# Attention projections: seven-product Strassen in float32 against three-pass Karatsuba in float32r, on one core

## The chip, the cores and the metric

The kernel runs on one core of one Trainium2 chip. The metric is the device time of one execution in microseconds (us). A core has a matrix engine (TensorE, in the profile PE, with its weight loads as PEld), a vector engine (VectorE, DVE), an engine for activation functions (ScalarE, ACT), a general engine (GpSimd, POOL) and SyncE (SP), which here only issues DMAs. Each of them works through its own queue in order and waits for others by semaphores. Matrix products land in PSUM[...] and are read out from there by VectorE or ScalarE; all other tiles lie in SBUF.

## The reference

64 graphs share one adjacency matrix `a` of 256 x 256 nodes; `x` is 64 x 256 x 512, float32. Two layers, each with a residual and a layer norm:

```python
# layer 0
mi = x @ Wi.T ; mj = x @ Wj.T
x = layernorm(x + deg * (mi + b) + a @ mj)
# layer 1
q, k, v = x @ Wq.T + bq, x @ Wk.T + bk, x @ Wv.T + bv      # 8 heads of 64
attn = softmax(where(a == 0, -inf, q @ k.T / 8))
x = layernorm(x + (attn @ v) @ Wo.T + bo)
```

Each of the four weights of layer 1 is 512 x 512. Per graph, each of these projections is a product of 256 x 512 with 512 x 512.

## The kernel before

**Batches in pairs.** The loop (`for g in range(NG - 1)`, L986) runs 31 times, with two graphs ("batches") per turn: it does the attention of pair `g`, layer 0 of pair `g + 1`, the output projection `o` of pair `g`, and q, k, v of pair `g + 1`. Layer 0 of the first pair and its q, k, v stand ahead of the loop; the attention and the output of the last pair follow it.

**Layer 0** (`l0_steps`, L502) is a Strassen scheme over the two row tiles and two halves of the channels: seven products per batch, each of two float32 matmuls with 512 columns, in the banks `x`, `w`, `y` and `z`. The left factors are the transposed input `xT` (`turn_x`, a VectorE transpose) and its four combinations `xS` (`sum_x`, L494). Steps 5 to 7 give `mj`, which is split into a float32r head `hi` (ScalarE) and a rest `lo` (GpSimd). `neighbours` multiplies both by the adjacency matrix `graph`, in eight float32r matmuls per batch, into the two banks of `pa`. `take` adds the result to `xh` and begins the norm, `give` applies it.

**h is turned through DRAM.** `send_h` (L599) writes the two row tiles of the normed rows to DRAM in two DMAs; after the second one it issues the read of the whole batch into `hB`. `turn_h` (L610) transposes 128 x 1024 at once on VectorE into `hT`, and for the second batch forms the four combinations `hS`.

**Projections before** (`pair_steps`, L650; `block_product`, L640). The two batches of a pair are the two row blocks of a Strassen scheme: seven products, each of four float32 matmuls with 256 columns, for each of q, k, v (`qkv_steps`, L675) and o (`o_steps`, L737). The right factors are 128 x 512 blocks or combinations of blocks (256 KB each), made once ahead of the loop (`make_factors`, L412), kept in DRAM and streamed in by `bring` (L438) through a ring of nine buffers; a factor that has been used is replaced by the next at once. Products are evicted by ScalarE (copies) and joined by VectorE and GpSimd (`u1`, `u2`, `u3`).

**Attention.** A slot `w` is a pair of heads of one batch. `scores` (L795) computes scores for a slot (4 matmuls) and returns a function that adds the mask (VectorE, L809), takes the exponential (ScalarE, L813) and adds the two key tiles for the denominators (GpSimd, L816). `values` (L830) multiplies by v. `divide_two` (L850) copies two slots out and calls `divide` (L875): denominators by a matmul with ones, the reciprocal (VectorE, L886), eight small DMAs that spread the reciprocals over the partitions, and a running sum `rtot` on GpSimd. `multiply` (L845) applies them on GpSimd later.

**PSUM.** `score_banks` are two buffers of two banks each; they hold scores, and `pa` of the neighbour sum. `value_bank` is one bank, and `bank` is a pool of three. Together they are all eight.

**What sets the order.** Instructions given to `in_order` (L282) keep the order of the program on their engine; that holds for all matmuls. The others are placed by the compiler's scheduler. Before, many of VectorE's and GpSimd's instructions were free in this sense, the mask add among them. Matmuls are all recorded under L290, their helper's line.

## Time and profile before

| | |
|---|---|
| median of 3 runs | 3070.68 us (3068.39 to 3071.82) |
| the profiled execution | 3068.79 us |
| its span in the profile | 3066.9 us |
| granted TensorE clock, mean | 0.999 of full |
| weights and activations moved by DMA | 447.54 MB, 146 GB/s on average |
| DMA queue of SyncE, share of 16 engines | 48.8% |

The costliest groups of TensorE, by name of the tile written and the tiles read (a float32 matmul is two records, so counts are twice the number of matmuls; busy times overlap with those of neighbours):

| group | shape | records | busy us |
|---|---|---|---|
| layer 0, `po` from `w0` and `xS` or `xT` | 128 x 512 | 1792 | 814.3 |
| projections, `st` from `factor` and `hS`, `hT`, `oS` or `aoT` | 128 x 256 | 7112 | 1625.1 |
| scores, `ps` | 64 x 256 | 2048 | 265.0 |
| values, `pav` | 128 x 256 | 4096 | 248.4 |
| neighbour sum, `pa` | 128 x 512, float32r | 512 | 212.2 |

In the views below a row of a timeline has the start in us from the beginning of the span, the length, the engine, the line, the operation, output and inputs, the shape, and the number of records that were merged into the row. Brackets name the time that the engine was idle before it, and what ended it. A row of the waits names who waited, for whom, the total, the number of times and the longest one.

### The profile page before, as it was taken

What the parts mean: (1) busy time and instruction counts of PE and PEld (TensorE: products, weight loads), DVE (VectorE), ACT (ScalarE), POOL (GpSimd) and SP (SyncE); (2) the same over time, 40 slices, a digit from 0 to 9 for tenths busy, and PEclk for the clock granted to TensorE, in tenths of its full rate; (3) what the DMA queues carried; (4) which work ended last, traced back from release to release, by engine and by line L of the source; (5) the groups of instructions that cost most, each with busy time, mean ns of one, the idle gap of its engine ahead of it and who ended that gap; (6) DMA issues with size and microseconds to landing.
All of it is one profiled execution on the core that took longest, in us unless ns stands there. A gap on an engine that the chain in (4) does not pass through costs nothing. (4 is left out here: it accounts for less than half of the span.)

```text
span 3066.9 us, 46810 instructions
## 1 busy us (share of the span) xinstructions
PE 3036.6 (99%) x16646; PEld 2124.6 (69%) x16646; DVE 2178.3 (71%) x3298; ACT 974.1 (32%) x1861; POOL 1519.5 (50%) x1255
## 2 busy tenths in 40 slices
PE   7999999999999999999999999999999999999998
PEld 4667766677766777666776667776677766677665
DVE  6776677766777667777677777677766777767775
ACT  2323333323333333332233332333333333323332
POOL 2544545544545445464454554454544546445453
PEclk9999999999999999999999999999999999999999
DMA  7455544455444555345553445544455444555333
GB/s 255 123 151 159 169 121 136 132 161 166 144 125 127 159 170 155 116 133 154 161 168 119 126 145 160 167 134 134 127 158 170 151 121 128 159 161 166 120 111 96
DMA packets 410411, 447.54 MB, mean 146 GB/s; under 512 B 40896, under 2 KB 300224, under 8 KB 409792
## 3 DMA queue, kind: packets, MB, share of 16 engines
q1 hardware_dynamic: 410176, 444.50, 48.8%
q8 instruction: 136, 2.23, 0.3%
q14 instruction: 99, 0.81, 0.1%
HBM read 340.79 MB, written 70.25 MB: 134 GB/s over the span
## 5 line engine op out<-in xcount | busy, mean ns | idle before, releaser
L461 POOL TENSOR_TENSOR rstd<-ve,mhalf 128x1 f32<-128x1 f32 x256 | 140.5, 552 | 707.3 <-DVE below L459 707.3
L816 POOL TENSOR_TENSOR pk<-pe 128x512 f32<-128x512 f32 x256 | 323.1, 1278 | 322.2 <-ACT pe L813 322.2
L290 PE MATMUL po<-w,xS 128*128 128x512 f32 x1024 | 462.2, 599 | 0.7 <-DVE xS L478 0.7
L290 PE MATMUL st<-hS,factor 128*128 128x256 f32 x2048 | 453.2, 379 | 1.5 <-DVE u L689 1.2
L290 PEld LDWEIGHTS st<-hS,factor 128*128 128x128 f32 x2048 | 388.4, 190 | 56.3 <-DVE xh L744 1.7
L813 ACT ACTIVATE pe<-pe 128x1024 f32<-128x1024 f32 x256 | 270.8, 1058 | 364.4 <-DVE pe L809 364.4
L290 PE MATMUL po<-w,xT 128*128 128x512 f32 x768 | 352.1, 601 | 14.8 <-DVE xS L477 9.3
L290 PE MATMUL st<-hT,factor 128*128 128x256 f32 x1536 | 352.5, 379 | 0.7 <-ACT hT L626 0.7
L290 PEld LDWEIGHTS po<-w,xS 128*128 128x128 f32 x1024 | 189.6, 190 | 235.6 <-issue 206.3
L809 DVE TENSOR_TENSOR pe<-ps,maskT 128x1024 f32<-128x1024 f32 x256 | 298.0, 1195 | 35.4 <-PE ps L290 35.4
L290 PEld LDWEIGHTS st<-hT,factor 128*128 128x128 f32 x1536 | 291.9, 190 | 41.8 <-ACT hT L626 0.9
L886 DVE RECIPROCAL rden<-den 128x256 f32<-128x256 f32 x127 | 222.5, 1752 | 76.6 <-PE den L290 73.6
L290 PEld LDWEIGHTS po<-w,xT 128*128 128x128 f32 x768 | 144.2, 191 | 181.9 <-issue 162.8
L887 POOL TENSOR_TENSOR rtot<-rtot,rden 128x256 f32<-128x256 f32 x127 | 106.8, 841 | 320.1 <-DVE rden L886 320.1
L290 PE MATMUL ps<-qT,kT 64*128 64x256 f32 x2048 | 265.0, 393 | 0.0
L290 PE MATMUL pav<-pe,v_sb 128*32 128x256 f32 x4096 | 248.4, 382 | 1.9 <-ACT pe L813 1.9
L290 PEld LDWEIGHTS ps<-qT,kT 64*128 64x128 f32 x2048 | 184.5, 186 | 78.1 <-issue 38.6
L744 DVE TENSOR_TENSOR xh<-st,xh 128x512 f32<-128x512 f32 x186 | 144.5, 777 | 132.2 <-PE st L290 132.2
L290 PE MATMUL st<-factor,hS 128*128 128x256 f32 x1024 | 234.8, 382 | 0.0
L290 PEld LDWEIGHTS pav<-pe,v_sb 128*32 128x32 f32 x4096 | 119.8, 110 | 164.3 <-issue 95.4
L290 PE MATMUL st<-factor,oS 128*128 128x256 f32 x992 | 224.2, 379 | 0.0
L290 PEld LDWEIGHTS st<-factor,hS 128*128 128x128 f32 x1024 | 192.1, 190 | 35.2 <-issue 10.6
(115 smaller groups left out, 4648.2 us busy)
## 6 DMA issues: line engine op xcount, KB each, us to landing
xB<-in_x_dram SPq DMA_DIRECT2D x256, 128.0 KB, 3.9
xh<-in_x_dram SPq DMA_DIRECT2D x64, 512.0 KB, 4.2
factor<-wq SPq DMA_DIRECT2D x128, 256.0 KB, 4.2
factor<-wk SPq DMA_DIRECT2D x128, 256.0 KB, 2.8
factor<-wv SPq DMA_DIRECT2D x128, 256.0 KB, 2.6
spread<-rden SPq DMA_DIRECT2D x1016, 32.0 KB, 1.9
factor<-wo SPq DMA_DIRECT2D x124, 256.0 KB, 3.2
h_cols<-xh SPq DMA_DIRECT2D x124, 256.0 KB, 3.0
```

Source lines behind the costliest of these rows:

```text
L290: in_order(nc.tensor.matmul(*args, **kw))
L461: nc.gpsimd.tensor_tensor(rstd, ve, mhalf, ALU.pow)
L744: nc.vector.tensor_add(dst, src, dst)
L809: nc.vector.tensor_add(pe.rearrange("p j t q -> p j (t q)"), ps.rearrange("p j t q -> p j (t q)"), maskT.rearrange("p t q -> p (t q)").uns ...
L813: in_order(nc.scalar.activation(flat, flat, AF.Exp, scale=QSCALE, accum_out=etot[:, NB * g + i, pr:pr + 1]))
L816: nc.gpsimd.tensor_tensor(pk, pe[:, :, 0, :], pe[:, :, 1, :], ALU.add)
L886: nc.vector.reciprocal(rden, den)
L887: nc.gpsimd.tensor_tensor(rtot, rtot, rden, ALU.add)
```

## The change

Its parts:

- **Projections in three float32r passes.** Each activation is split into a head, a low part and a difference (`split_head` on ScalarE, `split_low` on GpSimd, `split_diff` on VectorE), and each weight likewise (`make`): head, lifted low part, difference. The product is `X = head*head + low*lift` and `Y = diff*diff`; the result is `UP * X + Y`. Every projection is thus three products of full size, of float32r matmuls with 512 columns: 48 per projection and pair, and nothing is combined over the two batches. `hS`, `oS` and the keepers `u1` to `u3` go.
- **Weights** come in 16 chunks per turn (four for each weight) of 128 x 3 x 512, 786 KB each, through a ring of `RING = 6` buffers. Ahead of the loop a chunk is made by ScalarE and VectorE from the raw weight and stored.
- **Banks.** Each product takes a pair of banks (`pair`): "S" one of the two score buffers, "M" two of the pool of three, "A" one of these and the value bank.
- **v in pairs** (`v_pair`): both row tiles of a batch go through chunk by chunk. o goes row tile by row tile for the first batch, and in a pair for the second.
- **h in halves.** Each row tile is sent (`send_h`), fetched (`fetch_h`) and turned (`turn_h`) by itself.
- **Order.** Nearly every instruction is now given to `in_order`, and the loop's body is written out. Steps 1 to 4 of the next layer 0 are moved into the turn before.
- **Smaller ones.** `mj` is added by VectorE from PSUM instead of a copy and an add on GpSimd; the second `lo` of a batch is VectorE's; `rtot` is summed by ScalarE; the heads' channels are laid out so that `divide` needs four DMAs instead of eight.

The core of the diff:

```diff
-    AHEAD = 8
+    RING = 6
+    UP, DOWN, LIFT = 1 + 2.0 ** -12, 1 - 2.0 ** -13, 2.0 ** 12
...
+    def make(f, name, j):
+        head, lift, diff = (f[:, i, :].rearrange("p (c o) -> p c o", c=NC) for i in range(3))
+        low = p3.tile([P, NC, P], F32, tag="lu", name="low")
+        for cs, raw in pieces(name, j):
+            in_order(nc.scalar.activation(head[:, cs], raw, AF.Identity, scale=DOWN))
+            in_order(nc.vector.tensor_sub(low[:, cs], raw, head[:, cs].bitcast(F32)))
+            in_order(nc.scalar.activation(lift[:, cs], low[:, cs], AF.Identity, scale=LIFT))
+        in_order(nc.vector.scalar_tensor_tensor(diff, low, LIFT, head.bitcast(F32), ALU.mult, ALU.subtract))
+        nc.sync.dma_start(out=kept[name][j], in_=f.bitcast(F32))
...
+    def split_head(parts, src):
+        in_order(nc.scalar.activation(parts[0], src, AF.Identity, scale=DOWN))
+
+    def split_diff(parts, src):
+        in_order(nc.vector.scalar_tensor_tensor(parts[2], parts[0].bitcast(F32), UP, src, ALU.mult, ALU.subtract))
+
+    def split_low(parts, src, engine):
+        in_order(engine.tensor_tensor(parts[1], src, parts[0].bitcast(F32), ALU.subtract))
...
+    def pair(kind):
+        if kind == "S":
+            both = score_banks("pxy")
+            return both[:, 0, :], both[:, 1, :]
+        return bank("px"), value_bank("py") if kind == "A" else bank("py")
+
+    def rows_of_product(banks, parts, t, f, c):
+
+        X, Y = banks
+        head, low, diff = (d[:, c, t * P:(t + 1) * P] for d in parts)
+        first, end = c == 0, c == NC - 1
+        matmul(X, head, f[:, 0, :], start=first, stop=False, skip_group_check=True)
+        matmul(Y, diff, f[:, 2, :], start=first, stop=end, skip_group_check=True)
+        matmul(X, low, f[:, 1, :], start=False, stop=end, skip_group_check=True)
...
+    def v_pair(g, i, kinds, last):
+        def run():
+            if g not in vv:
+                vv[g] = p1.tile([P, NB, NT, D], F32, tag="v", name="v_sb")
+            banks = {t: pair(kinds[t]) for t in (1, 0)}
+            for c in range(NC):
+                for t in (1, 0):
+                    rows_of_product(banks[t], hP[g], NT * i + t, coming[0 if last else c], c)
+                if last:
+                    coming.pop(0)
+                    bring()
+            for t in (1, 0):
+                v_evict(g, i, t, banks[t])
+        return run
```

o for the second batch, with the fetches and turns of h inside it (`fetch` and `turn` are `fetch_h` and `turn_h` of the second batch of the next pair):

```diff
+        def two():
+            banks = [pair(kinds[NT + t]) for t in range(NT)]
+            for c in range(NC):
+                for t in range(NT):
+                    rows_of_product(banks[t], parts, NT + t, coming[0], c)
+                coming.pop(0)
+                bring()
+                if c in fetch:
+                    fetch[c]()
+            h1 = turn(1)
+            split_head(*h1)
+            split_low(*h1, nc.gpsimd)
+            add_x(1, 0, banks[0])
+            add_y(1, 0, banks[0])
+            split_diff(*h1)
+            h0 = turn(0)
+            split_head(*h0)
+            split_low(*h0, nc.gpsimd)
+            add_x(1, 1, banks[1])
+            split_diff(*h0)
+            add_y(1, 1, banks[1])
```

The loop's body, first and last thirds (`p` and `q` are the layer-0 steps of batches 1 and 2 of the next pair, counted from 0; `next_scores` computes two slots' scores, adds the mask of the first and returns the rest of the second):

```diff
+        run([p[4], p[5], q[0], p[6]])
...
+        values(g, 0)
+        values(g, 1)
+        sum_x(b2)
+        divide_two(g, 1)
+        next_scores(2)()
+        nb1()
+        add1(1)
+        add1(0)
+        run(q[1:2])
+        stat1(1)
+        run(q[2:3])
+
+        values(g, 2)
+        values(g, 3)
...
+        values(g, 6)
+        values(g, 7)
+        aoP[g][1], = three(("v",))
+        split_low(*ao_parts(g, 0, every), nc.gpsimd)
+        split_low(*ao_parts(g, 1, upper), nc.gpsimd)
+        divide_two(g, 7)
+        if g + 2 < NG:
+            next_p[0][2]()
+        split_diff(*ao_parts(g, 1, upper))
+        nb2()
+        add2(1)
+        add2(0)
+        stat2(1)
+        multiply()
+        split_head(*ao_parts(g, 1, lower))
+        give2(1)
+        send_h(b2, 1)
+        p, q = next_p, next_q
+        v, q_, k = projection_steps(g + 1)
         end = finish_steps(g)
...
+        o[0]()
+        stat2(0)
+        split_diff(*ao_parts(g, 1, lower))
+        split_low(*ao_parts(g, 1, lower), nc.gpsimd)
+        give2(0)
+        send_h(b2, 0)
+        o[1]()
+        run([o[2], v[0]])
+        sum_x(b3)
+        v[1]()
+        turn_x(b3 + 1)
+        run([end[0], q_[0], end[1], k[0], end[2], q_[1], end[3], k[1], end[4]])
...
+        run([q_[2]])
...
+        run([k[2], q_[3]])
+        run([scores(g + 1, 0), scores(g + 1, 1)])
+        if g + 2 < NG:
+            add_bias(b3 + 1)
+            p[0][3]()
+        k[3]()
```

## The prediction, made before the changed kernel was run

> **What bounds the kernel now.** I read the page first, then TensorE's list of waits, then the timeline of one turn of the main loop, engine by engine. From the page (busy time by engine) and from TensorE's waits:

> ```profile
> PE 3036.6 (99%) x16646; PEld 2124.6 (69%) x16646; DVE 2178.3 (71%) x3298; ACT 974.1 (32%) x1861; POOL 1519.5 (50%) x1255
> ...
> PE po L290 <- DVE xS L477: 9.3, 1, 9.3
> ```

> TensorE is busy 99% of the span, and its longest wait comes once, at the start. Busy can flatter (ends of matmuls are modelled), so I take starts instead. TensorE's timeline, with start, length and count of records:

> ```profile
> 1495.70 7.07 PE L290 MATMUL st<-hS,factor 128*128 128x256 f32 x32
> 1502.61 1.89 PE L290 MATMUL st<-factor,hT 128*128 128x256 f32 x8
> ...
> 1534.97 0.50 PE L290 MATMUL pa<-hi,graph 128*128 128x512 f32 x1
> 1535.31 0.40 PE L290 MATMUL pa<-lo,graph 128*128 128x512 f32 x1
> 1535.54 0.40 PE L290 MATMUL pa<-hi,graph 128*128 128x512 f32 x1
> ...
> 1536.72 0.39 PE L290 MATMUL pa<-lo,graph 128*128 128x512 f32 x1
> 1537.04 1.14 PE L290 MATMUL ps<-qT,kT 64*128 64x256 f32 x8
> ...
> 1629.37 0.50 PE L290 MATMUL pa<-hi,graph 128*128 128x512 f32 x1
> ```

> Three readings. One turn (same matmul to same matmul) takes 1629.37 - 1534.97 = 94.40 us. In a projection 32 records take 1502.61 - 1495.70 = 6.91 us, so a record of 256 columns costs 0.216; a float32 matmul is two records, 0.432. The float32r matmuls of the neighbour sum are one record each: (1536.72 - 1535.31) / 6 = 0.235 us for 512 columns. Entering and leaving such a run costs 0.2 more: 1537.04 - 1534.97 = 2.07 against 8 x 0.235 = 1.88.

> TensorE never starves because the others are ready in time, barely. VectorE around this neighbour sum and the next, and SyncE (DMA issue) after it:

> ```profile
> 1506.67 0.42 DVE L479 TENSOR_TENSOR xS<-xT 128x256 f32<-128x256 f32 x1
> ...
> 1534.05 1.76 DVE L886 RECIPROCAL rden<-den 128x256 f32<-128x256 f32 x1 [0.52 <-PE den L290]
> 1535.72 1.16 DVE L809 TENSOR_TENSOR pe<-ps,maskT 128x1024 f32<-128x1024 f32 x1
> 1537.14 0.69 DVE L579 TENSOR_TENSOR xh<-pa,xh 128x512 f32<-128x512 f32 x1 [0.26 <-PE pa L290]
> ...
> 1559.21 0.69 DVE L579 TENSOR_TENSOR xh<-pa,xh 128x512 f32<-128x512 f32 x1 [0.72 <-PE pa L290]
> ...
> 1575.90 2.10 DVE L485 STREAM_TRANSPOSE hT<-hB 128x1024 f32<-128x1024 f32 x1
> ```

> ```profile
> 1564.35 0.38 SPq L603 DMA_DIRECT2D h_cols<-xh  x1
> ...
> 1566.55 0.41 SPq L603 DMA_DIRECT2D h_cols<-xh  x1
> ...
> 1572.00 0.33 SPq L607 DMA_DIRECT2D hB<-h_cols  x1
> ```

> The mask add ends at 1536.88, and the scores that need its PSUM buffer start at 1537.04: no time is lost, because only one score product stands before the neighbour sum. The second neighbour sum ends at 1559.02; its rows go to DRAM, back, and through the transpose that ends at 1578.00: 19.0 us.

> [...] a float32 512-column product takes two records of 0.43 (0.86), the float32r one 0.235. [...] the trace has 216 per float32 pass but 235 for float32r, and I use 235. [...] The kernel owns all eight (two score buffers of two banks, one value bank, three others), so a new product waits for a read of an old one. [...] the last sum of xS took 1.50 us beside GpSimd's lo, 0.42 otherwise.

> **The change, part by part, per turn of the loop (31 turns).**

> 1. TensorE. Removed: four projections x 28 matmuls x 0.432 = 48.35. Added: four x 48 float32r matmuls x 0.235 (0.2335 in the second run) = 44.83. Runs of float32r go from two to three (first neighbour sum; second sum with o, v and most of q and k; the last k step), +0.2. Layer 0, scores, values and denominators keep their counts. Net -3.3 us, if TensorE is fed.

> 2. VectorE. Out: the combinations of hS and oS (8 x 0.69), the recombinations after q, k, v (14 instructions, 8.8), o's adds (4.7). In: one add per q and k step (8 x 0.69), four for v, eight for o, the differences (h 4 x 0.7, attention 4 x 0.7), two lows 1.6. By my sum 68 becomes about 74 us of some 91: not the bound on average. But all of it is now pinned in program order, and TensorE's waits depend on where it stands.

> 3. GpSimd loses mj, rtot and the recombinations and gains lows: 47 to about 43. ScalarE gains heads, evictions and totals: 30 to about 39. Both lie beside TensorE; on the path only at the places below. Uncovered, one low costs 1.4 and one head 0.6.

> 4. First new wait: the first neighbour sum. It now follows both score products of w = 2 and 3, which hold both score buffers, so it waits for the mask add of w = 2. From the turn's start (layer-0 step 5): steps 5, 6, the next batch's step 1 and step 7 take 4 x 1.73 and end at 6.92; values and denominators 9.23; two scores 11.16: TensorE is ready. VectorE: mj 7.1 to 7.75, ScalarE's hi to 8.45, low to 9.15 (pinned, so VectorE waits for hi), sum_x 1.6 to 10.75, reciprocal 1.67 to 12.4, mask add to 13.56. Stall 2.4. Behind it in TensorE's queue stand steps 2 and 3 of the next batch and values(2). Bounds: with sum_x out of the way the reciprocal alone starts at 9.4 and 1.0 is left; with a low stretched by GpSimd 3.2. I take 2.4.

> 5. Second new wait: batch 2's rows of h. After the second neighbour sum come o (48 matmuls), v of batch 1 (24): 72 x 0.235 = 16.9 us, then v of batch 2, which needs h of that batch; before, this chain took 19.0. New in it: the halves shorten the last transpose by 1.05; head, difference and the o evictions between add about 2.5 (0.65 + 0.65 + 0.65 + 0.6); o's second score buffer is freed only by an add queued behind both transposes, so even v's first tile waits for them. ScalarE's give also stands behind a head that waits for GpSimd's multiply. Sum 20.2: stall 3.3. Bounds: 0 if pinned order and earlier fetches of half rows bring the chain under 16.9; 5.5 if the fetch runs behind the new weight chunks (next point). I take 3.2.

> 6. Transfers. Weights: 16 chunks of 786 KB instead of 28 of 262 KB, 12.6 MB instead of 7.3 per turn; the mean goes from 146 to about 210 GB/s, while two-microsecond windows of this trace reach 374. Each q or k step eats a chunk in 2.8 us (279 GB/s), with six in the ring. I take no stall of its own. Spread DMAs fall from eight to four per pair on SyncE (gain on its queue: 4 x 0.6, beside TensorE). xB loads moved out of turn_x move along SyncE's queue, and each bring that waits for its slot holds what is behind it, h's fetches too; that is the upper bound in point 5.

> 7. Start: 12 chunks must be made by ScalarE and VectorE before or during the first projections; the first takes about 2.9 us (0.6 + 0.7 + 0.6 + 1), the next 1.5 each, against v's 0.7 per chunk: some 5 us lost, 2.6 won by three cheaper projections. +3, bounds -3 to +12. The tail keeps its products: 0.

> Sum: 31 x (-3.3 + 2.4 + 3.2) = 31 x 2.3 = +71, +3 at the start. The profiled execution took 3068.79 (span 3066.9); it becomes about 3143. The median is 1.9 above it, within the spread of the runs; I rounded the two stalls down a little and forecast 3140 for the median.

> **Rivals.**
> - Forecast (0.50): both new waits cost more together than the 3.3 won. 3085 to 3185.
> - The stream stays fed (0.25, faster): the h chain fits into 16.9 us, and only part of the first stall stays, 1.0. 31 x (-3.3 + 1.0) + 3 = -68: about 3002; with no stall at all 2971. For: TensorE waited for nothing in the middle of the trace, and SyncE's queue is shorter. Against: 19.0 us measured for the chain. Where both stalls together come under 3.3 us a turn, this side decides.
> - Weight transfers become the bound (0.20): h's write, fetch and the ring collide with 786 KB chunks, 2 us more a turn: 3140 + 62 = 3202. For: 302 to 374 GB/s in busy windows already; against: six chunks in the ring.
> - Gain and stalls cancel (0.05): 3070.

> **How the numbers follow.** A difference under 0.2% (6 us) can't be told from none. Faster 0.25 (the second case), same 0.04 (most of the last), slower 0.71 (first, third, rest). Predicted 3140. Low end 3005: it keeps half of the fed case, leaving about 0.11; high end 3205 leaves about 0.09. The likeliest case's own range is 3085 to 3185.

> **What would show it.** The float32r records of the projections 0.235 apart (point 1); turn length from neighbour sum to neighbour sum near 96.7; TensorE idle some 2.4 us before the first neighbour sum, released by the mask add L809's successor (point 4); idle some 3 us before batch 2's v, released by VectorE's add of o or GpSimd's low (point 5); VectorE busy near 80%. Wrong if TensorE runs through both places, if float32r products come 0.216 or 0.43 apart, or if SyncE's factor loads release TensorE.

## The result: slower by 9.5%, four times the predicted loss

The changed kernel takes 3359.93 us (median of 4 runs, 3357.99 to 3366.22) against 3069.6 for the kernel before: ratio 1.0948, 95% interval 1.0929 to 1.0967. Predicted were 3140 us, with a range of 3005 to 3205. The direction held, the size did not. The profiled spans are 3356.2 and 3066.9 us, 289.3 apart.

The page of the changed kernel, busy time by engine, then the granted TensorE clock in tenths, by slice of the span:

```profile
PE 3009.1 (90%) x15638; PEld 1952.3 (58%) x15638; DVE 2274.6 (68%) x3413; ACT 1204.8 (36%) x2247; POOL 1382.3 (41%) x1056
...
PEclk8999999999999999999999999999999999999999
```

TensorE was 99% busy before and is 90% busy now. No other engine is a bound on average: VectorE stands at 68%, not the 80% that I foretold. So TensorE waits, and its list of waits says for whom (us in all, times, longest):

```profile
PE pxy L290 <- DVE xh L747: 128.5, 31, 4.2
PE pa L290 <- DVE pe L816: 70.4, 31, 3.2
PE px L290 <- DMA factor<-wv: 42.4, 41, 1.9
PE pa L290 <- DVE lo L538: 36.8, 31, 1.5
PE px L290 <- POOL v L616: 19.1, 30, 0.6
```

Four of them come once in nearly each of the 31 turns, the one for `wv` 41 times; together they make 297 us, 9.6 a turn. None of them existed before. TensorE's timeline shows where they lie, in one turn and at the start of the next:

```profile
1482.65 1.16 PE L290 MATMUL pa<-hi,graph 128*128 128x512 f32 x4 [2.24 <-DVE pe L816]
...
1514.08 0.73 PE L290 MATMUL pa<-lo,graph 128*128 128x512 f32 x2 [1.17 <-DVE lo L538]
...
1517.41 0.39 PE L290 MATMUL px<-factor,qT 128*128 128x512 f32 x1
1517.64 0.39 PE L290 MATMUL py<-factor,kT 128*128 128x512 f32 x1
...
1532.59 0.50 PE L290 MATMUL px<-factor,hA 128*128 128x512 f32 x1 [1.20 <-DMA factor<-wv]
...
1538.38 0.77 PE L290 MATMUL pxy<-factor,hA 128*128 128x512 f32 x1 [4.14 <-DVE xh L747]
1538.94 0.63 PE L290 MATMUL pxy<-factor,hD 128*128 128x512 f32 x1
1539.37 0.63 PE L290 MATMUL pxy<-factor,hL 128*128 128x512 f32 x1
1539.80 0.63 PE L290 MATMUL px<-factor,hA 128*128 128x512 f32 x1
...
1585.54 1.15 PE L290 MATMUL pa<-hi,graph 128*128 128x512 f32 x4 [2.24 <-DVE pe L816]
```

I read starts, as in the prediction. This turn takes 1585.54 - 1482.65 = 102.9 us instead of 94.4. Products that have their inputs stand 0.227 apart (1517.41 to 1517.64, and over long stretches). After the 4.14 us wait they stand 0.43 apart. The DMA issues and VectorE at that place show what the wait is made of:

```profile
1525.81 0.33 SPq L637 DMA_DIRECT2D hB<-h_cols  x1
1526.24 0.38 SPq L441 DMA_DIRECT2D factor<-wv  x1
1526.71 0.38 SPq L441 DMA_DIRECT2D factor<-wq  x1
1527.19 0.38 SPq L637 DMA_DIRECT2D hB<-h_cols  x1
```

```profile
1535.12 1.13 DVE L496 STREAM_TRANSPOSE hF<-hB 128x512 f32<-128x512 f32 x1 [0.74 <-DMA hB<-h_cols]
...
1537.55 0.68 DVE L747 TENSOR_TENSOR xh<-pxy,xh 128x512 f32<-128x512 f32 x1
```

The second read of h, issued at 1527.19 behind weight chunks, has landed at 1535.12. Only then can VectorE turn it, and the add that empties o's last bank stands behind that in its queue. The windows of the same place add the clock (busy time of PE, PEld, DVE, ACT and POOL, then PEclk, DMA share, GB/s):

```profile
1533.00:1535.00 2.00, 1.24 (x6) 0.68 (x4) 1.38 (x2) 0.00 (x0) 0.82 (x1) 1.00 1.02 414
1535.00:1537.00 2.00, 0.00 (x0) 0.00 (x0) 1.72 (x3) 0.72 (x2) 0.01 (x1) 0.85 0.47 197
1537.00:1539.00 2.00, 0.62 (x2) 0.56 (x3) 2.00 (x4) 0.88 (x2) 1.76 (x1) 0.50 0.00 0
1539.00:1541.00 2.00, 2.00 (x6) 1.59 (x5) 1.86 (x5) 0.00 (x0) 0.00 (x0) 0.50 0.00 0
1541.00:1543.00 2.00, 2.00 (x6) 1.53 (x5) 0.00 (x0) 0.00 (x0) 0.00 (x0) 0.50 0.25 52
1543.00:1545.00 2.00, 2.00 (x9) 1.60 (x9) 0.00 (x0) 0.00 (x0) 0.00 (x0) 0.95 1.08 372
```

The DMA engines are full up to the second read's landing (414 GB/s). TensorE runs dry at about 1534.2, and when work is there again, its clock is at half. The trace's clock records have 41 such stretches (186.9 us in all; 2 with 8.9 us before). Of them 33, with 146.7 us, lie in the 30 turns from the first to the last second neighbour sum of the loop. TensorE was busy in 128.4 us of these, and half of that, 2.1 us a turn, is lost: an upper value, since ends of matmuls are modelled.

The whole difference, by stage: the first scores of the loop start 31.3 us later (89.67 before, 120.96 now). A turn, from second neighbour sum to second neighbour sum, has a mean of 102.65 instead of 94.43. Of this +8.2: products -4.8 (192 x 0.227 = 43.6 for 48.35), waits +9.6, half clock +2.1, and 1.3 for what is left. That rest lies between the products: outside of listed waits and half clock their starts are 0.227 apart in the median but 0.234 in the mean, and 192 times the difference is 1.3. From the first scores to the end of the trace the turns make 289.3 - 31.3 = 258 us, 31 x 8.3.

### The profile page after: what moved, and what is told of

The parts are those of the page before. It is cut to its first block, busy times and chain, and to the rows that moved or that the text cites. A ratio compares the mean times of both kernels' runs of the same rounds, so it can differ in the third digit from the quotient of the medians.

```text
span 3356.2 us, 42750 instructions
## 1 busy us (share of the span) xinstructions
PE 3009.1 (90%) x15638; PEld 1952.3 (58%) x15638; DVE 2274.6 (68%) x3413; ACT 1204.8 (36%) x2247; POOL 1382.3 (41%) x1056
## 5 line engine op out<-in xcount | busy, mean ns | idle before, releaser
L290 PE MATMUL po<-w,xS 128*128 128x512 f32 x1024 | 476.3, 603 | 1.4 <-DVE mj L564 1.0
L290 PE MATMUL po<-w,xT 128*128 128x512 f32 x768 | 366.3, 614 | 12.6 <-DMA w<-in_wiT_dram 9.4
L616 POOL TENSOR_TENSOR hL<-hF,hA 128x512 fp32r<-128x512 f32 x124 | 187.8, 1515 | 356.8 <-ACT hA L610 356.8
L290 PEld LDWEIGHTS po<-w,xS 128*128 128x128 f32 x1024 | 187.4, 190 | 231.1 <-issue 191.8
L496 DVE STREAM_TRANSPOSE hF<-hB 128x512 f32<-128x512 f32 x124 | 143.8, 1160 | 218.0 <-DMA hB<-h_cols 218.0
L701 DVE TENSOR_TENSOR kT<-py,kT 128x512 f32<-128x512 f32 x128 | 88.6, 692 | 261.9 <-ACT kT L700 261.9
L290 PE MATMUL ps<-qT,kT 64*128 64x256 f32 x2048 | 256.5, 389 | 0.0
L290 PE MATMUL pav<-pe,v_sb 128*32 128x256 f32 x4096 | 248.6, 382 | 5.0 <-ACT pe L820 3.0
L290 PEld LDWEIGHTS po<-w,xT 128*128 128x128 f32 x768 | 144.1, 194 | 182.3 <-issue 157.4
L906 DVE RECIPROCAL rden<-den 128x256 f32<-128x256 f32 x127 | 221.6, 1745 | 18.9 <-PE den L290 17.3
L290 PE MATMUL pxy<-factor,hA 128*128 128x512 f32 x256 | 115.7, 452 | 131.5 <-DVE xh L747 128.5
L290 PEld LDWEIGHTS ps<-qT,kT 64*128 64x128 f32 x2048 | 187.0, 186 | 69.3 <-PE pav L290 38.7
L610 ACT ACTIVATE hA<-hF 128x512 fp32r<-128x512 f32 x124 | 78.2, 630 | 399.6 <-DVE hF L496 399.6
L290 PEld LDWEIGHTS pav<-pe,v_sb 128*32 128x32 f32 x4096 | 119.5, 109 | 168.1 <-issue 71.9
L478 ACT ACTIVATE xh<-xh,shift,rstd 128x512 f32<-128x512 f32 x256 | 208.7, 815 | 8.5
L616 POOL TENSOR_TENSOR v<-aoT,qT 128x512 fp32r<-128x512 f32 (+1 forms) x93 | 184.4, 1996 | 0.0
L290 PE MATMUL px<-hA,factor 128*128 128x512 f32 x640 | 184.3, 410 | 0.0
L290 PE MATMUL py<-hD,factor 128*128 128x512 f32 x640 | 176.3, 397 | 5.1 <-ACT kT L700 5.1
```

What stands on the lines that cost most here:

```text
L290: in_order(nc.tensor.matmul(*args, **kw))
L478: order(nc.scalar.activation(t, t, AF.Identity, bias=shift, scale=rstd))
L496: in_order(nc.vector.transpose(dst.rearrange("p c (n a) -> p a c n", n=R), blocks.rearrange("p a (r c) -> p a c r", c=NC)))
L610: in_order(nc.scalar.activation(parts[0], src, AF.Identity, scale=DOWN))
L616: in_order(engine.tensor_tensor(parts[1], src, parts[0].bitcast(F32), ALU.subtract))
L701: in_order(nc.vector.tensor_add(dst, Y, dst))
```

## The experiments

"Turn" is the mean of 30 turns in the trace. "v" is the time of that stage; its 48 products at 0.227 are 10.9. "Half clock" sums all stretches of the clock records, those ahead of the loop too. The ratio is to the kernel before (3070 us, turn 94.43), with its 95% interval. The diffs are cut to their core ("..." marks what is left out), and times "after the second sum" count from its start, as medians of 26 turns.

| kernel | us | ratio | turn | v | half clock |
|---|---|---|---|---|---|
| changed kernel | 3359.9 | 1.0948 (1.0929 to 1.0967) | 102.65 | 19.15 | 187 |
| first sum between scores | 3345.9 | 1.0900 (1.0882 to 1.0918) | 102.29 | 19.79 | 237 |
| fetch first | 3316.0 | 1.0798 (1.0780 to 1.0816) | 101.38 | 17.07 | 163 |
| dummy products | 3346.1 | 1.0893 (1.0871 to 1.0914) | 102.32 | 18.39 | 134 |
| v row by row | 3241.0 | 1.0556 (1.0538 to 1.0574) | 98.91 | 14.80 | 84 |
| read out first | 3348.3 | 1.0899 (1.0881 to 1.0917) | 102.53 | 18.80 | 187 |
| transfers alone | 3397.6 | 1.1058 (1.1037 to 1.1080) | 103.86 | 19.65 | 258 |
| three orders | 3200.2 | 1.0428 (1.0411 to 1.0445) | 97.58 | 14.0 | 63 |
| + low on GpSimd | 3156.6 | 1.0279 (1.0261 to 1.0296) | 96.24 | 14.12 | 62 |
| + multiply early | 3163.2 | 1.0304 (1.0287 to 1.0321) | 96.25 | 14.65 | 71 |
| + send on ScalarE | 3186.4 | 1.0366 (1.0349 to 1.0383) | 97.47 | 15.9 | 146 |
| fetch after v | 3144.4 | 1.0238 (1.0221 to 1.0255) | 95.74 | 16.34 | 77 |
| fetch on ScalarE | 3124.0 | 1.0175 (1.0158 to 1.0192) | 95.03 | 15.67 | 110 |
| start | 3132.9 | 1.0194 (1.0176 to 1.0212) | 95.78 | 16.44 | 64 |
| start, fetch on ScalarE | 3109.7 | 1.0133 (1.0116 to 1.0150) | 94.89 | 15.54 | 108 |
| q and k chunks held | 3087.4 | 1.0058 (1.0041 to 1.0075) | 94.28 | 14.87 | 103 |
| layer 0 before v | 3128.5 | 1.0178 (1.0156 to 1.0200) | 95.77 | 15.02 | 72 |
| sends and hold | 3134.0 | 1.0210 (1.0192 to 1.0227) | 95.70 | 16.34 | 119 |
| sends, no hold | 3260.1 | 1.0610 (1.0593 to 1.0628) | 99.89 | 20.57 | 271 |

**First sum between scores.** The neighbour sum goes between the two score products, as it stood before:

```diff
-        next_scores(2)()
-        nb1()
+        scores(g, 2)()
+        nb1()
+        scores(g, 3)()
```

> Only the first neighbour sum is moved, between the two score products, as it stood before the change. Theory (TensorE waits there for VectorE's mask add because both score buffers are taken): the 2.27 us of idle per turn ahead of pa go, about 3360 - 31 x 2.2 = 3290. Rival (VectorE is the bound, and what is not waited for here is waited for at the next place): 3350 to 3365, with the idle time found again at the second neighbour sum or at v.

The wait for the mask add fell from 70.4 to 31.1 us, but the time only by 14, a little more than the rival allowed. The turn became 102.29, v grew by 0.6, and half clock rose by 50 us: in the middle of the trace it came at 1425.44, 1527.84 and 1630.24, each 102.4 us after the last, always in v. So the mechanism of this wait was right, but TensorE lost in v half of what it won here.

**Fetch first.** Both reads of batch 2's h behind the first freed weight slot:

```diff
-        o = o_steps(g, "SMAS", {0: lambda: fetch_h(b2, 1), 2: lambda: fetch_h(b2, 0)}, lambda t: turn_h(b2, t))
+        o = o_steps(g, "SMAS", {0: lambda: (fetch_h(b2, 1), fetch_h(b2, 0))}, lambda t: turn_h(b2, t))
```

> Both reads of batch 2's h are issued after the first weight chunk of o's last stage instead of the second one after three. Theory (h lands late because up to three chunks of 786 KB are ahead of it): the second half lands 3 to 4 us earlier, the 4.15 us of idle ahead of v of batch 2 fall below 1.5 and TensorE's clock is not halved after them; about 3360 - 31 x 5 = 3205. Rival (the transfers of this stretch are one sum, whatever their order): the weights come later by as much, TensorE waits for factor<-wv instead; 3330 to 3360.

The second read landed 20.1 us after the second sum instead of 24.3. The wait for `xh` ahead of batch 2's v fell from 128.5 to 70.6, the one for `wv` rose from 42.4 to 66.1. The time lies between theory and rival. A part of the wait is the place of a 262 KB read behind 786 KB chunks, and the chunks pay for it.

**Dummy products.** Ten products without use, put into a bank of row tile 0 ahead of batch 2's v, to keep TensorE busy in its wait:

```diff
-            banks = {t: pair(kinds[t]) for t in (1, 0)}
+            banks = {}
+            if last:
+                banks[0] = pair(kinds[0])
+                for n in range(10):
+                    matmul(banks[0][1], hP[g][0][:, 0, :P], coming[0][:, 0, :], start=True, stop=True,
+                           skip_group_check=True)
+            for t in (1, 0):
+                if t not in banks:
+                    banks[t] = pair(kinds[t])
```

> Ten matmuls whose result is overwritten are put ahead of v of batch 2, where TensorE idles; nothing else is touched, so h lands as late as before and v can't begin earlier. Theory (the half clock after this idle stretch comes from the stretch's length): the clock stays at 1.0, the 192-matmul run keeps 0.227 us per matmul, about 3360 - 31 x 2.1 = 3295. Rival (the half clock has another cause[...]): 3360 or a little over.

v fell by 0.8 a turn, the time by 14 instead of 65: the clock did not stay at full. Half clock fell by 53 us only. It still came in v in 18 of the 30 turns, where 60.3 us of the wait are left (1.9 a turn), and it came at the first neighbour sum, which waits 2.2 us, 10 times instead of 3: in the middle of the trace at 1477.90, 1580.30 and 1682.70. Keeping TensorE busy for a part of one wait doesn't cure it.

**v row by row** for the second batch, in place of `v_pair`:

```diff
+            for t in (1, 0):
+                banks = pair(kinds[t])
+                for c in range(NC):
+                    rows_of_product(banks, hP[g], NT + t, coming[0 if t == 0 else c], c)
+                    if t == 0:
+                        coming.pop(0)
+                        bring()
+                v_evict(g, 1, t, banks)
...
-            v = [v_pair(g, 0, "MS"[::-1], False), v_pair(g, 1, "AS", True)]
+            v = [v_pair(g, 0, "MS"[::-1], False), v_rows(g, "SA")]
```

> v of batch 2 goes one row tile after the other, the first one in the bank pair that comes free early, so it needs only the first half of h. Theory (v waits for the second half of h and for o's last bank pair): 12 matmuls (2.7 us) run before the second half is there, the idle time is split, no half clock; about 3360 - 31 x (2.5 + 2.1) = 3217. Rival (the first half and the weights are just as late): 3340 to 3360.

The largest gain of one edit: 119 us, near the theory's 143. Row tile 1 runs while row tile 0 is still on its way, and it takes the pair of banks that comes free early ("SA" for "AS"); the next experiment tests the bank alone. The wait that led the list is gone from TensorE's waits, and a smaller one for ScalarE's read of v's bank is new:

```profile
PE pa L290 <- DVE pe L828: 70.4, 31, 3.2
PE px L290 <- DMA factor<-wv: 49.6, 43, 2.1
PE pxy L290 <- ACT v_sb L707: 38.5, 30, 1.4
```

**Read out first.** VectorE adds o's last tile before the second transpose, not after it:

```diff
+            add_x(1, 1, banks[1])
+            add_y(1, 1, banks[1])
             h0 = turn(0)
...
-            add_x(1, 1, banks[1])
             split_diff(*h0)
-            add_y(1, 1, banks[1])
```

> The changed kernel with one edit: VectorE reads o's last tile out ahead of the second h's transpose instead of behind it. The wait for xh ahead of v of batch 2 there is 128.5 us in all, 4.1 a turn. Theory (the pair needs both tiles' h at once, so the second h's transfer is what it waits for): the wait changes its name, to hA or hD, and stays over 100 us; time within 10 of 3360. Rival (only the bank is late, the read-out being queued behind the transpose): the wait falls below 40, half clock after it goes; time 3220 to 3270.

```profile
PE px L290 <- DMA factor<-wv: 48.8, 45, 2.0
PE pxy L290 <- DVE xh L747: 41.7, 31, 1.7
PE pa L290 <- DVE lo L538: 36.7, 31, 1.5
PE px L290 <- ACT hA L610: 21.2, 31, 1.1
PE px L290 <- POOL v L616: 19.2, 30, 0.7
PE px L290 <- POOL hL L616: 18.4, 31, 0.6
```

The wait splits over bank, head and low part of h: 41.7 + 21.2 + 18.4 + 6.3 (hD) = 88 of 128.5 stay, and the time falls by 12. Both numbers lie a little outside the theory's (over 100 us, within 10 us), far from the rival's. The bank is late, but behind it the pair waits for the second row tile itself. So in v row by row it is the order of the rows, more than the bank, that gains.

**Three orders**: first sum between scores, fetch first and v row by row together, with `sum_x(b2)` moved behind step 3 of the next batch:

```diff
-        sum_x(b2)
         divide_two(g, 1)
...
         run(q[2:3])
+        sum_x(b2)
```

> Three orders together: first neighbour sum between the scores (and sum_x behind it), h fetched ahead of the weight chunks, v of batch 2 row by row. Theory (the loss is idle time at these places plus the half clock that follows idle time, and they hide one another when only one is mended): v falls from 19.2 to about 12.5 us a turn, no idle time ahead of pa, nearly no half clock; a turn of 95 us, about 3125. Rival (the effects of the single edits just add, 14 + 44 + 119 us): 3185. Second rival (VectorE or the transfers are the bound): above 3230.

**+ low on GpSimd**: on top of it, the low part that was VectorE's goes back to GpSimd, and GpSimd's low part of the attention is cut in two:

```diff
-                lambda: lows(0, nc.vector))
+                lambda: lows(0, nc.gpsimd))
...
-        split_low(*ao_parts(g, 0, every), nc.gpsimd)
+        for cs in (upper, lower):
+            split_low(*ao_parts(g, 0, cs), nc.gpsimd)
```

> c1, and the second low of layer 0 is made by GpSimd ahead of the lows of the attention, which are cut in two. Theory (VectorE's low took 2.9 instead of 0.7 us [...] and TensorE waits 1.2 us a turn for it): c1 - 31 x 1.2 = 37 us less. Rival (GpSimd is then late for o): no change, with the wait at o instead.

**+ multiply early** (multiply and head ahead of the second norm's sums) and **+ send on ScalarE** (both sends of batch 2 from ScalarE's queue), each on top of the last:

```diff
-        stat2(1)
         multiply()
         split_head(*ao_parts(g, 1, lower))
+        stat2(1)
+        split_low(*ao_parts(g, 1, lower), nc.gpsimd)
...
-        split_low(*ao_parts(g, 1, lower), nc.gpsimd)
```

```diff
-        send_h(b2, 1)
+        send_h(b2, 1, nc.scalar)
...
-        send_h(b2, 0)
+        send_h(b2, 0, nc.scalar)
```

> c2, and the last multiply and what hangs on it stand ahead of the norm's statistics. Theory (h's chain and o's lower half wait behind this multiply on GpSimd and ScalarE): o's wait for its low goes (0.6 us) and h is sent 1.5 us earlier; 30 to 60 us less than c2. Rival (h's chain is set by the transfers): 20 us less, from o's wait alone.

> c3, and h's two rows are sent from ScalarE's queue, so the weight chunk behind them on SyncE's queue is not held up. Theory (the wait for factor<-wv, 1.4 us a turn, comes from this order): 20 to 40 us less than c3. Rival (the chunks are late for lack of bandwidth): within 10 us of c3.

The three orders give 160 us of the 290. The single gains add to 177, so nothing shows that they hide one another. But the late `sum_x` makes a new wait of 54.5 us, for `u`, which blurs the sum. The low part on GpSimd gives 44 more, and the second neighbour sum falls from 3.76 to 2.26 us. Two waits fell by it: the one for VectorE's low part (38.3 us) is gone, and with GpSimd's long low part cut in two the one inside o went from 19.1 to 7.9. The changed kernel's VectorE and GpSimd timelines show what this edit removed:

```profile
1511.17 2.86 DVE L538 TENSOR_TENSOR lo<-mj,hi 128x512 fp32r<-128x512 f32 x1
...
1580.49 0.69 DVE L538 TENSOR_TENSOR lo<-mj,hi 128x512 fp32r<-128x512 f32 x1 [0.68 <-ACT hi L574]
```

```profile
1510.66 4.51 POOL L616 TENSOR_TENSOR v<-aoT,qT 128x1024 fp32r<-128x1024 f32 x2
```

The same instruction takes 0.69 us alone and 2.86 beside GpSimd's long low part. Multiply early shortened o from 12.0 to 11.44 us, v gave 0.5 back: no gain in time, which neither theory nor rival had. Send on ScalarE made it worse by 23 us, against both: the wait for `wv` became 102 us. With the sends gone from SP the first v chunk goes out 2.7 us earlier and the second send, now beside it, takes 4.0 us to land instead of 2.6. The second read of h waits for that send, and the last v chunk stands behind this read: it goes out 16.5 us after the second sum instead of 15.0.

**Fetch after v**, **fetch on ScalarE** and **start**, all on the multiply-early kernel with `sum_x(b2)` right after the third score product; fetch on ScalarE passes `nc.scalar` to both `fetch_h`. "Start" is fetch after v with the lift of a chunk put off in `make`, four of the first six `bring()` between layer 0's steps ahead of the loop, and the evictions of q, k and the last v tile ahead of `bring()`:

```diff
-        o = o_steps(g, "SMAS", {0: lambda: (fetch_h(b2, 1), fetch_h(b2, 0))}, lambda t: turn_h(b2, t))
+        o = o_steps(g, "SMAS", {1: lambda: (fetch_h(b2, 1), fetch_h(b2, 0))}, lambda t: turn_h(b2, t))
...
+        def end():
+            in_order(nc.scalar.activation(lift, low, AF.Identity, scale=LIFT))
+            nc.sync.dma_start(out=kept[name][j], in_=f.bitcast(F32))
+
+        lifts.append(end)
+        if len(lifts) > 1:
+            lifts.pop(0)()
```

> The multiply-early kernel (3163, 96.25 us a turn), with batch 2's two h fetches given to SP behind the last v chunk instead of ahead of it, and sum_x moved to just after the third score mask add. Theory (what is left per turn is waiting for transfers and for one VectorE sum): the wait for wv chunks, 58.6 us in all there, falls below 15, the wait for u (40.2) below 5, nothing new; turn 93.1, time 3065 (3045 to 3085). Rival (h is the tight transfer, whatever is sent ahead of it delays v of batch 2): the wait for hA or xh of batch 2 grows by 2 us a turn in their place, turn 95 or more, 3120.

> As the kernel with the fetches behind the last v chunk, but the two fetches issued from ScalarE's queue, so that neither they nor the chunks wait for each other in a queue. Theory (queue order is the matter, bandwidth not): wait for wv below 15 us and no wait for h above the multiply-early kernel's; turn 92.5 to 93.1, time 3045 to 3070. Rival (bandwidth is the matter: the 256 KB reads then share the engines with 768 KB chunks): wv or h waits of 1.5 us a turn stay, turn 94.5, 3110.

> As the kernel with the fetches behind the last v chunk, and in the start alone: four of the first six chunks made between layer 0's steps of the first two batches, each chunk's lift behind the next chunk's head, evictions ahead of the chunk making on ScalarE and VectorE. Theory (chunk making on ScalarE and VectorE in series holds the start): the loop's first scores begin 10 to 15 us earlier, time 10 to 15 us below that kernel's. Rival (the start is held by the layer-0 and normalisation chain or by loads): under 4 us.

> The mended start together with the fetches on ScalarE's queue. Theory: the two gains add, 3035 to 3060, under the 3070 of the kernel before the change. Rival: above 3076, that is, three float32r passes stay slower even with waits, queue order and start mended.

The wait for `u` (55.2 us in multiply early) is gone. Fetch after v missed its time by 80 us: the wait for `wv` fell from 79.7 to 34.5, but 43.2 us for hD and 26.6 for hA took its place; that is the rival. (The 58.6 and 40.2 of the expectation are of the stretch from 600 to 2800 us.) Fetch on ScalarE: `wv` 73.5, also the rival's reading. "Start" was right. In the changed kernel ScalarE makes a chunk in 1.9 us (some 2.0 for the first), idle while VectorE forms the low part in between:

```profile
54.71 0.62 ACT L448 ACTIVATE factor<-raw 128x512 fp32r<-128x512 f32 x1
56.16 0.63 ACT L450 ACTIVATE factor<-low 128x512 fp32r<-128x512 f32 x1 [0.83 <-DVE low L449]
56.70 0.62 ACT L448 ACTIVATE factor<-raw 128x512 fp32r<-128x512 f32 x1
58.07 0.63 ACT L450 ACTIVATE factor<-low 128x512 fp32r<-128x512 f32 x1 [0.76 <-DVE low L449]
```

With all parts of this edit the first scores start at 106.3 instead of 122.2, and the time falls by 11.4; which part gave how much was not tested. Both gains together missed the hoped-for 3060 by 50.

**q and k chunks held**: the first q and k chunks are asked for only when ScalarE has read two numbers from their slots, behind the head of the last row tile.

```diff
-                coming.pop(0)
-                bring()
+                slot = coming.pop(0)
+                if c < 2:
+                    bring()
+                else:
+                    slots.append(slot)
...
+            for slot in slots:
+                seen = small.tile([P, 1], F32, tag="seen", name="seen")
+                in_order(nc.scalar.copy(seen, slot[:, 0, :1].bitcast(F32)))
+                bring()
```

> The kernel with the mended start and the fetches on ScalarE's queue (3110, 94.9 us a turn, of which v takes 15.5 where 48 products at 0.227 are 10.9), with the first q and k chunks held back until batch 2's last head is made, so that v2, v3 and the two h reads have the transfers to themselves. Theory (the rest is five or six transfers asked for within 2 us: 3.7 MB at 390 GB/s take 9.4 us, and q and k's 1.6 MB among them are not needed yet): wait for wv 75 us falls to under 30, half clock in few turns, turn 92.5 to 93.3, time 3030 to 3065. Rival (v2, v3 and h alone are too much, or q's chunk comes late in turn): the sum of the waits for wv, wq and h stays above 60 us, time above 3085.

The best of all, 22 us gained, but not as the theory had it: `wv` stays at 74.7, and the time is the rival's. SP's queue and ScalarE's timeline of this kernel show what was overlooked:

```profile
1581.08 3.20 SPq L642 DMA_DIRECT2D h_cols<-xh  x2
1584.37 0.99 SPq L445 DMA_DIRECT2D factor<-wv  x2
```

```profile
1583.06 0.82 ACT L488 ACTIVATE xh<-xh,shift,rstd 128x512 f32<-128x512 f32 x1
```

The second send waits for the norm's last step, to 1583.9, and both v chunks stand behind it. Hence two more, with the sends on ScalarE's queue too:

> The kernel with the q and k chunks held (3087, 94.3 us a turn, v 14.9), with batch 2's two h sends issued from ScalarE's queue too. Theory (v2's fetch waits on SP behind the second send, which waits for the norm: in that kernel it went out at 1584.4 although its slot was free at about 1581): v2 goes out some 3 us earlier, the wait for wv (75 us) falls to under 20, half clock in fewer turns; turn 91.8 to 92.6, time 3005 to 3035. Rival (with v2 and v3 earlier the h reads come later): a wait for hA or xh of batch 2 of 1.5 us a turn takes its place, time above 3065.

> As the kernel with sends and fetches on ScalarE's queue and the q and k chunks held, but q and k's first chunks asked for as soon as their slots are free. Theory (once v2 and v3 go out early, holding q and k back still matters to the h reads behind them): 10 to 25 us over the kernel that holds them. Rival (holding is worth nothing then): within 5 us of it.

The theory named the queue rightly, and the rival decides the time. TensorE's waits with sends and hold:

```profile
PE px L290 <- ACT hA L620: 46.5, 32, 1.7
PE py L290 <- DVE hD L623: 43.2, 31, 1.4
...
PE px L290 <- DMA factor<-wv: 8.7, 16, 1.6
```

The wait for `wv` is nearly gone, and 90 us of waiting for h replace it. Without the hold it is 160.2 for hA alone, and 126 us more time: far more than the 10 to 25 of the theory, and the rival's "nothing" is ruled out.

**Transfers alone**: fetches on ScalarE's queue and the hold, on the changed kernel itself.

> The changed kernel itself (3360, v 19.2 us a turn), with only the transfers of this stage reordered: h fetches on ScalarE's queue, first q and k chunks held back; v in pairs and all else as in the change. Theory (transfers are half of v's loss of 8.3): v falls to 15 or less, time 3225 to 3260. Rival (v in pairs needs batch 2's h 5.4 us after o whatever the order, and half clock follows): v 17 or more as with the fetches alone put first, time 3300 to 3320.

It is slower by 38 us, outside of both ranges. The pair's wait for `xh` grew from 128.5 to 157.0. In this order the last v chunk goes out ahead of the first read of h, which lands 21.4 us after the second sum instead of 19.6; the second one lands earlier, 22.1 for 24.3, but its transpose then stands behind the first one's work. So this order does not bring back half of v's loss with v in pairs; the order of "fetch first" did help there, by 44 us.

**Layer 0 before v**: one layer-0 product moved between o and v, on the kernel with q and k chunks held:

```diff
-        if g + 2 < NG:
-            next_p[0][1]()
...
-        run([o[2], v[0]])
+        o[2]()
+        if g + 2 < NG:
+            p[0][1]()
+        v[0]()
```

> The kernel with the q and k chunks held, with one layer-0 product of the next turn (4 matmuls, 1.8 us) moved from after the last scores to between o and v. Theory (what is left in v is transfers asked for too late, which any other TensorE work there covers): v with that product in it grows by less than 0.8, the stretch it left shrinks by 1.8, turn 91.3 to 92.3, time 3000 to 3035. Rival (the product covered the exponentials where it was): wait of values for pe grows by 1.5 a turn, time within 10 of the kernel without the move.

The wait for `wv` fell to 2.5 us, as meant. But the bank that follows waits 60.1 us for VectorE's add of the moved product, and the second neighbour sum, with less work ahead of it, takes 3.21 instead of 2.26. It is slower by 41 us, which neither theory nor rival had.

None of these beats the kernel before. In the best, the turn is as long as before (94.28 against 94.43); what is left, 1.0058, stands outside the turns: the second neighbour sum of the loop's first turn comes 17.3 us later, and 6.0 are lost after that of its last turn. Its v still takes 4.0 us more than its products. A ring with a seventh buffer was not tried.

## Why the prediction was wrong in size

The direction was right, and so were the two places where TensorE was to wait. The step that failed is the sum of what a turn loses. It had two waits, put the rest "beside TensorE" (point 3) or at "no stall of its own" (point 6), and had no term for the clock. A turn was to grow by 2.3 us and grew by 8.2. Of the 6 that were missing, the two foreseen waits are 0.8 (6.4 measured, 5.6 predicted), three waits put at nothing are 3.2 (1.2 for VectorE's low part, 1.4 for `wv`, 0.6 for GpSimd's low part in o), and half clock is up to 2.1. The start (point 7) adds 28 us once. Point by point:

- **Point 1, TensorE's content: about right, for the wrong reason.** -3.3 predicted. I took 0.235 from the short neighbour sum; the sum of -3.3 holds only with the 0.2335 beside it, and with 0.235 it is -3.0. Long runs have 0.227, which would give -4.8, but the mean of 0.234 leaves -3.4. That the two agree is luck.
- **Point 2: right that VectorE is no bound.** It stands at 68%, and a part of the damage comes from its pinned order, as points 3 and 4 show. Its sum is off: the terms listed add 2 us to 68, not 6, and the turn shown has 70.2.
- **Point 3: wrong in "beside TensorE".** The low part given to VectorE (point 2 had "two lows 1.6") stands right ahead of the second neighbour sum, and is stretched there to 2.86 us. The wait is 36.8 us. I knew of such a stretch and applied it only as the upper bound of the first sum. TensorE's wait for GpSimd's low inside o adds 19.1. Low on GpSimd ended the first and shortened the second, and gave 44 us.
- **Point 4: right**, 2.4 predicted, 70.4 / 31 = 2.27 measured. With the sum between the scores 31.1 / 31 = 1.0 was left. It only looks like the lower bound, which had `sum_x` out of the way; there `sum_x` stayed where it was.
- **Point 5: right place, right releaser (VectorE's add of o), too small.** 3.2 predicted, 4.15 measured. The chain from the end of the second neighbour sum to batch 2's v was put at 20.2 (its own terms make 20.5) and took 23.9; the wait is not longer because TensorE itself came there 2.7 us later than the 16.9 predicted. What was the upper bound, a fetch behind weight chunks, was the case: the second read took 7.6 us to land (the whole batch took 3.7 before), and fetch first cut the wait to 70.6. The sum also assumed a chain of rows; the pair of row tiles in v, which needs both h tiles at once, was not in it. v row by row shows it: 119 us.
- **Point 6: the "no stall of its own" failed.** `wv` costs 1.4 a turn, and more once others go (75 us in the best version). The mean (182 GB/s; I said about 210, but the bytes given there make some 195) doesn't show it: four chunk slots come free within the last 5.5 us of o, and chunks, sends and reads of h all want the engines then (414 GB/s). Each order that I tried moved the wait from one to another.
- **No point had the half clock**, up to 2.1 us a turn. The trace has it in each of the 30 turns, at the wait ahead of batch 2's v (4.14 us in the turn shown, then products 0.43 apart instead of 0.227). That it follows the waits is shown by v row by row (187 to 84 us). The 2.2 us wait of the first sum drew it too, but less often (in 3 turns of the changed kernel, in 10 with dummy products); the last section has what the clock records show of this.
- **Point 7: the term furthest off in proportion.** +3 predicted, bounds to +12; 31.3 measured. I priced a chunk at 1.5 us after the first, it takes 1.9, and the evictions of q and k stand behind the making in ScalarE's queue. The edit "start" brought the first scores 16 us forward and the time 11.4 down; the cause of the rest stays open.

In numbers: 31 x 2.3 + 3 = 74 predicted, 258 + 31 = 289 measured. The rival of weight transfers as the bound named one of the missing parts; no rival had several of them at once, with the clock on top.

## What to carry to other kernels

A fully busy engine hides that its suppliers have no slack: a shorter stage pulls every due time behind it forward, so list for each what must be there at the new time, before counting the products saved. A wait that recurs each turn on TensorE is to be priced with the half clock that the traces show behind it (here up to 2.1 us a turn, most of it behind a wait of 4.1; see the last section), and an edit that ends one wait is to be judged by the turn, not by that wait. Where bulk chunks and small urgent transfers come due in the same few microseconds, look at the order of each issuing queue, sends included, and at the bytes due in that window, not at the mean rate.
